# A graph-attention layer and a top-p attention layer on one core: layer 1 put in order by a list scheduler at build time instead of written plans, with the buffers at the seam of the layers shared

## The chip, the core and the metric

The kernel runs on 1 core of one Trainium2 chip. The metric is the device time of one execution in microseconds (us). Five queues run side by side: PE (matrix products), DVE and ACT (element-wise work), POOL (small column work) and SP, which here only issues DMAs. Each queue runs its own instructions in order and waits on semaphores for the others. The inputs' transposed adjacency is laid out before the launch.

## The reference

There are N = 3327 nodes with D = 256 features and a symmetric 0/1 adjacency matrix. Two pre-normalised layers follow each other:

```python
# layer 0: graph attention, 4 heads of 64 features
h = relu(layernorm(x))
support = h @ weight                      # per head
w = leaky_relu(f1[m] + f2[n], 0.2) on the edges; attn = softmax over neighbours
x = x + attn @ support + bias + h @ proj_w.T + proj_b
# layer 1: two steps of a row-normalised graph sum R and of top-p attention A
X = relu(layernorm(x));  R = (adj + eye) / row sums
for n in range(2):
    A = top_p(softmax((Xa @ W1.T @ W2.T) @ (Xa @ W3.T).T), 0.9)   # rows cut to 90% of the mass, renormalised
    Xf = R @ Xf;  Xa = A @ Xa
    Z += Xf @ U1[n].T + Xa @ U2[n].T
x = x + layernorm(X + Z) * ln_g + ln_b
```

`A` is N x N and dense before the cut, so both steps make all 3327 x 3327 logits, find each row's threshold and multiply the cut matrix with `Xa`.

## The kernel before

Rows are cut into NT = 26 tiles of 128 (the last has 127). Layer 0 walks the adjacency in four column blocks of 6, 8, 8 and 4 tiles (`BLOCKS`), and within each over the 26 row tiles j; it makes attention weights on DVE (L588), sums features and weights on PE (L596, L606), and writes each adjacency tile it has read to a DRAM copy `adj_r` from POOL's queue, which layer 1 reads. When a block ends, its output tiles (class `Out`) are divided, normalised, turned (transposed), made into keys and queries, and multiplied with `U1` (`graph`, L524) to give the rows `xf` of layer 1's graph sum. The outputs of blocks 0 to 2 run between the next block's products; those of the last block run in a loop after the main loop (L700 to L720), where only they are at work.

Layer 1 has two steps s. In each, each row tile i goes through this chain (`Rows`):

- logits in 7 pieces of 512 columns (PE, L826) into three PSUM banks, copied to `lg` by ACT or DVE (`evict`, L837);
- `exp` (ACT, L849), a first `guess` of the threshold (POOL), four probes (ACT, L907: a whole row each, with its sum), each followed by small steps on ACT and DVE (`aim`, `go_on`, `narrow`), then `threshold`;
- on DVE `low` (L964), `largest` (L973), `last_kept`, and `keep` (L1012), which cuts the row; `make_sure` on POOL;
- in 7 groups g of four column tiles: transposes on PE (L1025), copies by ACT or DVE (L1035), products with the features `xa` into one bank (PE, L1046);
- in step 0: scale, transpose, query and key of the next step, the small products with `U2` (L1089) and stores to DRAM; in step 1: norm and output.

Beside that runs the graph sum, 26 tiles x 7 parts a step: a part loads four 128x128 tiles of `adj_r` into one of three `adjt` buffers (SP, L748) and multiplies them with `xf`, as a high and a low half (L769, L770). When a tile's seven parts are done, `add`, and in step 0 `high` and `low`, finish it.

What a step needs of the one before: the keys of all tiles (the first 24 come back from DRAM in one load, the last two are put in directly), all `xf` rows for any graph part, and all `xa` rows for any product. The four `xf` buffers are reloaded in place from POOL's queue (`load_graph`), once step 0's graph sum is finished.

The order in layer 1 is written out: `PLANS` holds three lists for each step (for the first tiles, the middle, and the last), each a row of words such as `m.evict.v.2` (role, operation, engine, piece). A loop over n from -3 to NT + 2 walks the list; the roles sit at fixed distances (`ROLES`: m is a tile ahead, c two behind), so that one pass of the list serves several tiles. The word `graph` takes parts of the graph sum at a rate that `PARTS` sets: 3, 7 and 8 parts in the first passes of step 0, and 6, 10 and 7 in those of step 1. `in_traced_order` (L127) then ties PE, DVE, ACT and POOL to the order in which the program was written; SP's DMAs are not tied, and the tile framework places them.

```python
ROLES = {"m3": -3, "m2": -2, "m": -1, "a": 0, "b": 1, "c": 2, "d": 3}
PARTS = ({-3: 0, -2: 0, -1: 3, 0: 7, 1: 8}, {-3: 0, -2: 0, -1: 6, 0: 10, 1: 7})
for s in range(STEPS):
    for n in range(-3, NT + 3):
        plan = plans[0 if n < 2 else 1 if n < NT else 2]
```

Layer 0 and layer 1 have SBUF and PSUM pools of their own: layer 1's are opened when layer 0's are closed.

Of the kernel before, what the change touches and what calls it, by code (L numbers as in the profile page):

```python
# [21 lines left out]
P = 128  # L22
D = 256
# [27 lines left out]
ROOT = 1 / 64  # L51


@with_exitstack
def kernel(
# [71 lines left out]
    def in_traced_order(begin):  # L127


        last = {}  # L130
        for ins in nc.cur_bb.bb.instructions[begin:]:
            if ins.engine not in ORDERED:
                continue
            if ins.engine in last:
                tc.add_manual_dep(
                    ins,
                    last[ins.engine].name,
                    mybir.DependencyInfo(
                        mybir.DependencyClass.NoSync, mybir.DependencyReason.DATA
                    ),  # L140
                    reason="traced order",
                )
            last[ins.engine] = ins
# [45 lines left out]
    def queries_and_keys(xt, i, s, ptag, keys):  # L189
# [10 lines left out]
        yield from hi_and_lo(t, pq, i, s)  # L200
        nc.sync.dma_start(
# [7 lines left out]
    def new_keys(pool):  # L209
        k_sb = pool.tile([2 * DA, N + 1], FR, tag="k_sb", name="k_sb")  # L210
        return k_sb, small.tile([2 * DA, 2], FP, tag="mean", name="mean")
# [16 lines left out]
    def load_graph(pool, s):  # L228
        xf = new_graph(pool)
        for g0, g1 in SPREADS:  # L230
            if s == 0:
                ones_of_graph(xf, g0, g1)
            for t0, t1 in ((g0, min(g1, NF)), (max(g0, NF), g1)):
                if t0 < t1:
# [3 lines left out]
                    for v in range(2):  # L238
                        move_rows(
                            nc.gpsimd,  # L240
                            xf[b][:, c : c + t1 - t0, v * DX : v * DX + D].bitcast(FP),
                            xf_d[s][n0:n1, v].rearrange("(t p) d -> p t d", p=p), p,
                        )
        return xf

    def part_of_keys(s, part):
        n = (EARLY if s else BLOCKS[-1][0] - 2) * P
        return ((0, n), (n, N))[part]
# [17 lines left out]
    def mean_of_keys(keys, s, part):  # L266
# [4 lines left out]
            mean[:, part : part + 1], k_sb[:, n0:n1].bitcast(FP), AX.X, ALU.add  # L271
        )
        if part == 1:
            nc.vector.tensor_scalar(
                k_sb[:, N:], mean[:, :1], mean[:, 1:], 1.0 / N, ALU.add, ALU.mult
            )

    EARLY = NT - 2

    def load_u(pool):  # L280
        u_sb = pool.tile([P, DC, 2, D], FP, name="u_sb")
# [26 lines left out]
    keys = new_keys(right)  # L308
    first_traced = len(nc.cur_bb.bb.instructions)
    with ExitStack() as l0:  # L310
        p0 = l0.enter_context(tc.tile_pool(name="p0", bufs=1))
        pa = l0.enter_context(tc.tile_pool(name="pa", bufs=2))
        ps = l0.enter_context(tc.tile_pool(name="ps1", bufs=1, space=PSUM))

        def bank(k, shape):
            return ps.tile(shape, FP, tag=f"b{k}", name="pt")

# [31 lines left out]
        sup = p0.tile([P, NT, D], FP, name="sup")  # L349
# [22 lines left out]
        def normalize(i):  # L372
            normed[i] = hn = pa.tile([P, D], FP, tag="x1", name="hn")
# [4 lines left out]
        def turn(i, k):  # L378
# [6 lines left out]
            hT = pa.tile([P, DC, P], FP, tag="hT", name="hT", bufs=4)  # L385
# [3 lines left out]
        def features(i, k):  # L389
# [9 lines left out]
            if i == t0:  # L399
                made["ef"] = pa.tile([H, 4, P], FP, tag="ef", name="ef", bufs=1)  # L400
            nc.scalar.activation(eas[:, i], f1, AF.Exp, scale=SLOPE)
            nc.scalar.activation(cf[:, i], f1, AF.Exp, scale=1.0 - SLOPE)
            nc.scalar.activation(made["ef"][:, i - t0], f2, AF.Exp, scale=SLOPE - 1.0)
            if i == t1 - 1:
                spread(t0, t1, made["ef"])
# [26 lines left out]

        class Out:
# [10 lines left out]
            def normalize(r):  # L444
# [5 lines left out]
                x1 = pa.tile([P, D], FP, tag="x1", name="x1")  # L450
# [33 lines left out]
            def turn(r, k):  # L484
# [6 lines left out]
                r.hT = pa.tile([P, DC, P], FP, tag="hT", name="hT", bufs=4)  # L491
# [28 lines left out]
            def graph(r, k):  # L520
# [10 lines left out]
                move_rows(nc.sync, p_d[r.n0 : r.n0 + pn], xu, pn)  # L531

            def take_graph(r):
# [6 lines left out]
                ones_of_graph(xf0, i, i + 1)  # L540
                for v in range(2):
# [6 lines left out]
        HP = H // 2  # L548
# [5 lines left out]
        for c in range(DC):  # L554
            for v, row in enumerate((u_row, v_row)):
                t = pa.tile([P, D], FP, tag="x1", name="wx")
# [14 lines left out]
        w1n = p0.tile([DA, DC, P], FP, name="w1n")  # L571
# [9 lines left out]
        def weigh(j, at, b, cn, *heads):  # L581
            pj = rows(j)
            for h in heads:
                ws[h] = w = pa.tile([P, CH], FP, tag="w", name="w", bufs=7)
# [29 lines left out]
        def load_adj(b, j):  # L614
            c0, pj = BLOCKS[b][0] * P, rows(j)
            cn = min(BLOCKS[b][1] * P, N) - c0
            ats[b, j] = at = pa.tile([P, CH], FP, tag="at", name="at", bufs=4)
# [11 lines left out]
        for step, (b, j) in enumerate(order):  # L629
# [41 lines left out]
            ot = pa.tile([P, HP + 1, CH], FP, tag="ot", name="ot", bufs=1)  # L671
# [5 lines left out]
            if b < NB - 1:  # L677
                last = b == NB - 2
                for k, r in enumerate(outs):
# [10 lines left out]
                    for when, f in (  # L690
                        (a + 1, r.output),
                        (a + (5 if last else 4), lambda r=r: (r.take_keys(), r.store_keys())),
                        (g + 1, r.take_graph),
# [6 lines left out]
        mean_of_keys(keys, 0, 0)  # L700
        n = len(outs)
        free = [3, 4, 5, 6, 7, 0, 1, 2]
        for k, r in enumerate(outs):
            r.divide(free[k])
        for k in range(n + 2):
            if k < n:
                outs[k].normalize()
            if 0 <= k - 2:
                outs[k - 2].keys(free[k - 2])
            if k < n:  # L710
                outs[k].relu()
            if 0 <= k - 2:
                outs[k - 2].take_keys()
            if 0 <= k - 1 < n:
                outs[k - 1].turn(free[n + k - 1])
        for k, r in enumerate(outs):
            r.graph(free[n + k])
            r.take_graph()
            r.store_keys()
            r.store()  # L720


    pl = ctx.enter_context(tc.tile_pool(name="pl", bufs=1))
    lng = row_of(pl, ln_g, "lng")
    lnb = row_of(pl, ln_b, "lnb")

# [10 lines left out]
    def graph(i, s, xf, ends):  # L737


        pn, n0 = rows(i), i * P  # L740
        acc = ps.tile([P, DX], FP, tag="accr", name="accr")
        dx = D if s else DX
        for g in range(NG):
            c0 = 4 * g
            a = pw.tile([P, 4, P], FR, tag="adjt", name="adjt", bufs=ADJ)
# [10 lines left out]
            if g == 3:  # L756
                while ends:
                    ends.pop(0)[1]()
                ad = pw.tile([P, D], FP, tag="ad", name="ad", bufs=1)
                move_rows(nc.sync, ad, (z_d if s else p_d)[n0 : n0 + pn], pn)  # L760

            todo = [(a[: rows(c0 + j), j, :pn], c0 + j) for j in range(cn)]
            if g == 0:
                todo.insert(0, (ident_r[:pn, :pn], i))
            for n, (w, c) in enumerate(todo):
# [3 lines left out]
                nc.tensor.matmul(acc[:pn, :dx], w, xc[:, :dx], start=begin, stop=False)  # L769
                nc.tensor.matmul(acc[:pn, :D], w, xc[:, DX:], start=False, stop=end)  # L770
            if g < NG - 1:
                yield

        def add():
            if s == 0:
                nc.vector.reciprocal(rdeg[:pn, i : i + 1], acc[:pn, D : D + 1])
            nc.vector.scalar_tensor_tensor(
                ad[:pn], acc[:pn, :D], rdeg[:pn, i : i + 1], ad[:pn], ALU.mult, ALU.add
            )
            if s == STEPS - 1:  # L780
                move_rows(nc.sync, r_d[n0 : n0 + pn], ad, pn)

        def high():
            nc.scalar.copy(hl[:pn, 0], ad[:pn])

        def low():
            nc.vector.tensor_tensor(hl[:pn, 1], ad[:pn], hl[:pn, 0].bitcast(FP), ALU.subtract)
            move_rows(nc.sync, xf_d[s + 1][n0 : n0 + pn], hl.bitcast(FP), pn)

        ends.append(("dve", add))  # L790
        if s < STEPS - 1:
            hl = pw.tile([P, 2, D], FR, tag="hl", name="hl", bufs=1)
            ends += [("act", high), ("dve", low)]
        yield
# [3 lines left out]
    class Rows:  # L798
# [6 lines left out]
        def __init__(r, i, s):  # L805
            r.i, r.s, r.pn, r.n0 = i, s, rows(i), i * P
# [12 lines left out]
        def logits(r, k_sb, *pieces):  # L819
            pn = r.pn  # L820
            for p in pieces:
# [9 lines left out]
        def evict(r, copy, *pieces):  # L831
            for p in pieces:
                if p == 0:
                    r.lg = pw.tile([P, N + 1], FP, tag="lg", name="lg", bufs=3)
# [4 lines left out]
        def exp(r):  # L839
            pn = r.pn  # L840
            sc = small.tile([P, 13], FP, tag="sc", name="sc", bufs=4)
# [6 lines left out]
            r.e = pw.tile([P, N], FP, tag="e", name="e", bufs=3)  # L848
# [4 lines left out]
        def guess(r):  # L853
# [8 lines left out]
            r.ends = small.tile([P, 2, 2], FP, tag="ends", name="ends", bufs=4)  # L862
            r.at = small.tile([P, 5], FP, tag="at", name="at", bufs=4)
# [25 lines left out]
        def aim(r, j):  # L889

            pn = r.pn
            r.ea = small.tile([P, 1], FP, tag="ea", name="ea")
            nc.scalar.activation(r.ea[:pn], r.at[:pn, 4:], AF.Exp, bias=r.c2[:pn], scale=-1.0)
            r.aims = []
            for by in (BELOW[j],) if j < PROBES - 1 else (BELOW[j], NEAR):
                aim = small.tile([P, 1], FP, tag="aim", name="aim")
# [5 lines left out]
        def probe(r):  # L902

            pn = r.pn
            r.g = small.tile([P, 1], FP, tag="g", name="g")
            junk = pw.tile([P, N], F8, tag="junk", name="junk", bufs=1)
# [13 lines left out]
        def narrow(r, j):  # L920
# [12 lines left out]
            mk = small.tile([P, 2], U32, tag="mk", name="mk")  # L933
# [7 lines left out]
            t = small.tile([P, 4], FP, tag="t", name="t")  # L941
# [13 lines left out]
        def threshold(r):  # L955
            r.th = small.tile([P, 1], FP, tag="th", name="th")
# [4 lines left out]
        def low(r):  # L961
            pn, e = r.pn, r.e[: r.pn]
            r.below = small.tile([P, 1], FP, tag="below", name="below")
# [11 lines left out]
        def last_kept(r):  # L975
# [3 lines left out]
            top = small.tile([P, 1], FP, tag="top", name="top")  # L979
# [16 lines left out]
            r.vm = small.tile([P, 2], FP, tag="vm", name="vm")  # L996
# [12 lines left out]
        def keep(r):  # L1009
            pn, e = r.pn, r.e[: r.pn]  # L1010
            kept = small.tile([P, 1], FP, tag="kept", name="kept")
# [3 lines left out]
            r.rk = small.tile([P, 1], FP, tag="rk", name="rk", bufs=4)  # L1015
# [14 lines left out]
        def copy_transposed(r, copy, *groups):  # L1030
            for g in groups:
                pt = r.pt.pop(g)
                r.wt[g] = wt = pw.tile([P, 4, P], FP, tag="wt", name="wt", bufs=WT)
# [60 lines left out]
        def store_features(r):  # L1094
            y = pw.tile([P, D], FP, tag="y_or_x1", name="y", bufs=1)
            nc.scalar.copy(y[: r.pn], r.pz[: r.pn, 1])
            move_rows(nc.sync, xa_d[r.s + 1][r.n0 : r.n0 + r.pn], y, r.pn)

        def store_sum(r, xa):
            zt = pw.tile([P, D], FP, tag="nxa_or_rt", name="zt", bufs=1)  # L1100
# [403 lines left out]
```

## Time and profile before

| | |
|---|---|
| median of 3 runs | 2077.71 us (2077.64 to 2079.32) |
| profiled execution | 2080.33 us, of which the span from first to last instruction is 2078.5 |
| PE / weight loads / DVE / ACT / POOL busy | 1988.8 / 1391.1 / 1710.0 / 1271.3 / 790.6 us |
| mean granted PE clock | 0.981 |
| layer 0's main loop ends | 656 us |
| first exp and first transpose of layer 1 | 689.9 and 738.0 us |
| last A product of step 0 ends, first transpose of step 1 | 1398.7 and 1456.8 us |
| last A product of step 1 ends | 2068.1 us |

The busy share is an average over stages with different limits, and PE's busy time is modelled with overlapping matmuls, so the stages have to be read one by one. In rows of the form "engine line operation out<-in", L is a line of the kernel; a bracket gives the idle time before the instruction and what ended it.

### The profile page before, as it was taken

Reading aid. Unit: us, or ns where it says so; the run is one execution under the profiler, and the core shown is the slowest. Engines: PE = TensorE matmul, PEld = TensorE weight load, DVE = VectorE, ACT = ScalarE, POOL = GpSimd, SP = SyncE. Lnnn points to the kernel's source line nnn. Section 1 sums busy time; section 2 is a strip of 40 time slices with the busy share of each in tenths; the row PEclk is TensorE's granted clock in tenths of the full one; section 3 lists DMA queues with packets and bytes.
Section 4 is the critical chain, followed back from the end, with each engine's and each line's share of the span. In section 5 each row is a group of like instructions: output and inputs, shape, how many; then the busy total and the mean of one; then the engine's idle time right before and its main releaser. Section 6 shows DMA issues by size and latency. Waiting matters only on the chain.

```text
span 2078.5 us, 34250 instructions
## 1 busy us (share of the span) xinstructions
PE 1988.8 (96%) x11474; PEld 1391.1 (67%) x11474; DVE 1710.0 (82%) x4055; ACT 1271.3 (61%) x1950; POOL 790.6 (38%) x1860
## 2 busy tenths in 40 slices
PE   7999999999998689999999999997999999999996
PEld 3343333233223578888888888876798898888885
DVE  5767888988886488888888888855899999999985
ACT  2110100101112788888888888838899999999982
POOL 3221231223332244444444444423554445544441
PEclk9999999999998899999999999999899999999998
DMA  5455556565564433333333333377244343344320
GB/s 180 140 163 175 196 191 226 168 217 191 171 190 138 136 86 101 102 96 99 103 98 103 102 100 103 102 220 206 64 105 117 104 108 95 101 106 111 99 74 20
DMA packets 318881, 270.60 MB, mean 130 GB/s; under 512 B 30200, under 2 KB 293879, under 8 KB 318568
## 3 DMA queue, kind: packets, MB, share of 16 engines
q1 hardware_dynamic: 304024, 216.04, 37.7%
q0 software_dynamic: 13504, 51.62, 7.0%
q8 instruction: 92, 1.51, 0.3%
q14 instruction: 93, 0.76, 0.1%
q10 hardware_dynamic: 1168, 0.67, 0.1%
HBM read 177.79 MB, written 88.62 MB: 128 GB/s over the span
## 4 chain that ended last, share of the span: by engine, by line
PE 49%; ACT 12%; DVE 3%; issue 2%; DMA 1%; POOL 0%; SPq 0%; ACTq 0%; DVEq 0%; POOLq 0%
PE acca L1046 23%; ACT junk L907 7%; PE pt L1025 6%; PE pg L826 6%; PE accr L769 5%; PE accr L770 5%; ACT e L849 2%; PE pz L1089 2%; DMA adjt<-adj_r 1%; ACT lg L837 1%; ACT aim L897 1%; DVE v L973 1%; ACT wt L1035 1%; PE pq L195 0%; PE pt L524 0%
## 5 line engine op out<-in xcount | busy, mean ns | idle before, releaser
L907 ACT ACTIVATE junk<-lg,at 128x3327 fp8e4<-128x3327 f32 (+1 forms) x208 | 637.8, 3067 | 13.0 <-POOL at L873 10.6
L588 DVE SCALAR_TENSOR_TENSOR w<-xf,cf,at 128x1024 f32<-128x1024 f32 (+4 forms) x416 | 425.6, 1078 | 52.3 <-PE pt L606 51.7
L769 PE MATMUL accr<-xf,adjt 128*128 128x258 f32 (+3 forms) x1352 | 367.8, 305 | 19.1 <-DMA adjt<-adj_r 15.3
L770 PE MATMUL accr<-xf,adjt 128*128 128x256 f32 (+1 forms) x1352 | 341.9, 285 | 0.0
L596 PE MATMUL pt<-w,sup 128*64 128x512 f32 (+5 forms) x1456 | 337.5, 576 | 1.1 <-DVE w L588 1.0
L1046 PE MATMUL acca<-xa,wt 128*128 128x256 f32 (+2 forms) x1352 | 317.9, 384 | 2.9 <-ACT wt L1035 2.9
L1046 PE MATMUL acca<-res,wt 128*128 128x256 f32 (+2 forms) x1352 | 317.8, 380 | 0.0
L769 PEld LDWEIGHTS accr<-xf,adjt 128*128 128x128 f32 (+1 forms) x1352 | 260.0, 192 | 29.5 <-DMA adjt<-adj_r 18.9
L1046 PEld LDWEIGHTS acca<-xa,wt 128*128 128x128 f32 (+2 forms) x1352 | 252.2, 192 | 36.0 <-ACT wt L1035 3.9
L1046 PEld LDWEIGHTS acca<-res,wt 128*128 128x128 f32 (+2 forms) x1352 | 247.7, 190 | 30.4 <-issue 0.7
L770 PEld LDWEIGHTS accr<-xf,adjt 128*128 128x128 f32 (+1 forms) x1352 | 260.8, 193 | 5.7
L826 PE MATMUL pg<-k_sb,q 128*128 128x512 f32 (+2 forms) x728 | 243.4, 427 | 15.4 <-DVE lg L837 6.7
L596 PEld LDWEIGHTS pt<-w,sup 128*64 128x64 f32 (+1 forms) x1456 | 95.2, 136 | 206.7 <-issue 136.8
L847 POOL TENSOR_SCALAR sc<-sc 128x1 f32<-128x1 f32 (+1 forms) x156 | 29.3, 216 | 510.1 <-ACT sc L845 510.1
L1025 PE MATMUL pt<-ident,e 128*128 128x128 f32 (+1 forms) x1352 | 194.5, 277 | 19.2 <-DVE e L1012 13.5
L973 DVE MAX8 v<-lg 128x8 f32<-128x416 f32 (+2 forms) x416 | 209.9, 577 | 0.1
L1025 PEld LDWEIGHTS pt<-ident,e 128*128 128x128 f32 (+1 forms) x1352 | 163.9, 145 | 60.1 <-ACT wt L1035 17.1
L964 DVE SCALAR_TENSOR_TENSOR lg<-e,th 128x3327 f32<-128x3327 f32 (+1 forms) x52 | 191.1, 3676 | 4.2 <-ACT th L957 4.2
L1012 DVE SCALAR_TENSOR_TENSOR e<-e,vm 128x3327 f32<-128x3327 f32 (+1 forms) x52 | 191.2, 3678 | 0.1
L1035 ACT COPY wt<-pt 128x512 f32<-128x512 f32 (+2 forms) x268 | 142.7, 545 | 57.9 <-PE pt L1025 41.2
L849 ACT ACTIVATE e<-lg,sc 128x3327 f32<-128x3327 f32 (+1 forms) x52 | 159.7, 3072 | 29.4 <-issue 26.9
L606 PE MATMUL pt<-w,eas 128*32 128x512 f32 (+5 forms) x1456 | 166.6, 568 | 0.0
(179 smaller groups left out, 2660.1 us busy)
## 6 DMA issues: line engine op xcount, KB each, us to landing
adjt<-adj_r SPq DMA_DIRECT2D x300, 256.0 KB, 3.1
at<-in_adj_t_dram SPq DMA_DIRECT2D x50, 512.0 KB, 5.9
adj_r<-at POOLq DMA_DIRECT2D x50, 512.0 KB, 5.3
at<-in_adj_t_dram SPq DMA_DIRECT2D x25, 384.0 KB, 3.2
adj_r<-at POOLq DMA_DIRECT2D x25, 384.0 KB, 3.5
qk_d<-qk SPq DMA_DIRECT2D x50, 128.0 KB, 2.2
q<-qk_d SPq DMA_DIRECT2D x100, 64.0 KB, 2.5
xf_d<-xf SPq DMA_DIRECT2D x50, 128.0 KB, 3.8
```

Source lines behind the costliest of these rows:

```text
L588: nc.vector.scalar_tensor_tensor(o, cb, cf[:pj, j, h : h + 1], a, ALU.max, ALU.mult)
L596: nc.tensor.matmul(acc[q * O : (q + 1) * O, :mn], sup[:pj, j, h * O : (h + 1) * O], ws[h][:pj, 512 * m : 512 * m + mn], start=(j == 0), st ...
L769: nc.tensor.matmul(acc[:pn, :dx], w, xc[:, :dx], start=begin, stop=False)
L770: nc.tensor.matmul(acc[:pn, :D], w, xc[:, DX:], start=False, stop=end)
L826: nc.tensor.matmul(r.pg[p][:pn, :mn], r.q[:, v, :pn], k_sb[:, m0 : m0 + mn], start=(v == 0), stop=(v == 1),)
L849: nc.scalar.activation(r.e[:pn], r.lg[:pn, :N], AF.Exp, bias=nmu[:pn], accum_out=r.ssum[:pn])
L907: nc.scalar.activation(junk[:pn], r.lg[:pn, :N], AF.Exp, bias=r.at[:pn, 4:], accum_out=r.g[:pn], saturate=False,)
L964: nc.vector.scalar_tensor_tensor(r.lg[:pn, :N], e, r.th[:pn], e, ALU.is_lt, ALU.mult, accum_out=r.below[:pn])
L973: nc.vector.max(r.v8[:pn, q], r.lg[:pn, q * w : min((q + 1) * w, N)])
L1012: nc.vector.scalar_tensor_tensor(e, e, r.vm[:pn, 1:], e, ALU.is_ge, ALU.mult, accum_out=kept[:pn])
L1025: nc.tensor.transpose(r.pt[g][: rows(c), j, : r.pn], r.e[: r.pn, c * P : c * P + rows(c)], ident[: r.pn, : r.pn],)
L1046: nc.tensor.matmul(r.acc[: r.pn], wt[: rows(c), j, : r.pn], xa[: rows(c), c, :], start=(c == 0), stop=(c == NT - 1),)
```

## The change

The written plans, `ROLES`, `PARTS` and the loop over them are gone. A class `Order` holds all operations of layer 1, both steps together, as tasks: the engines that can do each with a duration, what it depends on, the buffers that it takes from a ring and what gives them back, a latency to its users, and a priority (tile number plus an offset for its kind, `PLACES`). DMAs are tasks of SP. `run` is a greedy list scheduler: among the ready tasks it takes the earliest start, and among equal starts the smallest priority; a copy that ACT or DVE can do goes to whichever ends it first. The kernel is then emitted in the order of the planned starts, and from the end of layer 0's main loop on SP is tied to that order too. Graph parts have priorities that trail their tile (`TRAIL`).

The resulting order, by the built program: 31 graph parts stand before the first transpose of layer 1, 169 of 182 before the first product of step 0's tile 25; the other 13, and nine of step 1, stand between the last product of step 0 and the first transpose of step 1; in step 1, 178 stand before the products of tile 24. Between them the logits of the first four tiles of step 1 are made (six pieces before the last products of step 0). ACT does 521 copies out of PSUM of layer 1 in place of 470, DVE 259 in place of 310.

The end of layer 0 is written out by hand as `end_of_layer_0`: the first two tiles' logits, exp and guess are interleaved with the last four outputs, whose stores move behind their key transfers. For that, the buffers of layer 1 exist from the start and layer 0 uses them as its own: `lg` and `spare`/`weights`, `sup` and the `e` buffers, `at4` (adjacency rows) and `wt`, `junk`, `ad`, `u_sb`. One set of eight PSUM banks (`Banks`) serves both layers. `hT` has two buffers in layer 0 for four. `xf`'s reload is cut by block (`load_block`) and issued from SP; each block waits for the graph parts that use it. Small column tiles have 5 buffers. The loads of `ln_g` and `ln_b` come late in step 0.

```diff
+PLACES = {"E": -2.11, "M": 0.88, "SF": 0.93, "AD": 1.14, "TH": 0.98, "LS": 2.27, "F": 0.18, "A": -0.7, ...
+TRAIL = (2.7, 0.49)
+PATIENCE = {"PE": 0, "DVE": 0, "ACT": 0.15}
+class Order:
...
+        R = dict(q=3, lgb=3, lgs=3, e=3, tr=2, wt=3, acca=1, accr=2, adjt=3, ad=1, hl=1, nxa=1, y=1, xaT=1, qks=1)
...
+                    A(K("L", x), [("PE", 0.46 if x < 6 else 0.26)], d, pr(s, i, "L"), take=[("lgb", K("L", x), [K("E", x)])] + ...
+                    A(K("E", x), [("ACT", 0.50 if x < 6 else 0.3), ("DVE", 0.61 if x < 6 else 0.36)], [K("L", x)] + ([K("E", 0)] if x else []), pr(s, i, "E"))
+                A(K("X"), [("ACT", 3.3)], [K("E", x) for x in range(NP)] + ([("X",) + before] if before else []), pr(s, i, "X"), take=[("e", K(), [K("T", g) for g in range(NG)])])
+                A(K("G"), [("POOL", 3.7)], [K("X")], pr(s, i, "G"))
+                A(K("P", 1), [("ACT", 3.08)], [K("G")], pr(s, i, "P"))
...
+                    A(K("AL", g), [("SP", 0.45 if g < 6 else 1.3)], [], pr(s, i, "GP") + p.lag[s] - 1 + g * 0.001, take=[("adjt", K("AL", g), [K("GP", g)])], lat=2.7, order=[pal])
...
+                    A(K("GP", g), [("PE", (0.97 + (0.25 if g == 0 else 0)) if g < 6 else 0.5)], [K("AL", g)] + ([prev] if prev else []) + xd, pr(s, i, "GP") + p.lag[s] + g / 7,
...
+            e = min(cands, key=lambda z: min(c[0] for c in cands[z]))
+            m = min(c[0] for c in cands[e])
+            lim = m + tol.get(e, 0.0)
+            c = min((c for c in cands[e] if c[0] <= lim + 1e-9), key=lambda c: (c[1], c[0]))
...
+    slots = {
+        "lg": list(lgs),
+        "e": [both[:, k * (N + 1) : k * (N + 1) + N] for k in range(2)],
+        "adjt": [adjt[:, k] for k in range(3)],
...
-        for k in range(n + 2):
-            if k < n:
-                outs[k].normalize()
...
-    PLANS = (
...
+        def end_of_layer_0():
+            first, second = (new_tile(0, i) or tiles[0, i] for i in (0, 1))
+            for g in range(3):
+                sums[0, 0].load(g)
...
+            outs[0].normalize()
+            for p in range(3):
+                logits(first, p, "s")
+            outs[1].normalize()
+            outs[0].relu()
+            for p in (3, 4):
+                logits(first, p)
...
+            outs[0].graph(4)
+            logits(first, 5, "s")
+            outs[1].graph(5)
+            for part in (1, 2):
+                mean_of_keys(keys, 0, part)
+            logits(first, 6, "v")
+            first.exp()
...
+            outs[2].graph(6)
+            logits(second, 4, "s")
...
+        begun = len(nc.cur_bb.bb.instructions)
+        end_of_layer_0()
+        l0.close()
...
+        order = Order(PATIENCE, TRAIL, offs=PLACES)
+        order.run(*tail_state())
+        for _, key, engine in order.order:
...
+            emit(key[0], engine, *key[1:])
+        in_traced_order(first_traced, ORDERED)
+        in_traced_order(begun, (E.SP,))
```

## The prediction

> **What bounds the kernel now.** I read the page's busy rows first, then the stretches of 40 us, then the chain of waits, and last the order of time around the three places where the stretches sag. Page: the engines' shares, PE's busy tenths, the granted clock.
>
> ```profile
> span 2078.5 us, 34250 instructions
> PE 1988.8 (96%) x11474; PEld 1391.1 (67%) x11474; DVE 1710.0 (82%) x4055; ACT 1271.3 (61%) x1950; POOL 790.6 (38%) x1860
> ...
> PE   7999999999998689999999999997999999999996
> ...
> PEclk9999999999998899999999999999899999999998
> ```
>
> PE looks full everywhere, but its busy time overlaps (matmul ends are modelled), so I pace it: each form costs its start-to-start step in the dense stretch. An A product (L1046) steps 0.216 us, a graph matmul (L769, L770) 0.12, a logits matmul 0.23, a transpose 0.11, a small product (L1089) 0.43. Counting instructions at these steps gives 1293 us of PE work in the 1422.5 us after 656 (end of layer 0's main loop). The other 129.6 are PE idle or at a low clock: 49.0 in 656 to 800, 37.3 in 1345 to 1500, 17.1 in 1500 to 2000, 26.5 after; nothing in 820 to 1340. The stretches (PE, PEld, DVE, ACT, POOL busy, clock, DMA) show the same three sags:
>
> ```profile
> 680.00:720.00 40.00, 25.08 (x123) 19.64 (x122) 13.91 (x45) 28.14 (x34) 13.90 (x50) 0.89 0.53 141
> ...
> 1000.00:1040.00 40.00, 40.00 (x239) 34.62 (x239) 34.81 (x94) 36.12 (x54) 17.05 (x48) 1.00 0.39 103
> ...
> 1440.00:1480.00 40.00, 30.53 (x158) 25.48 (x159) 32.18 (x89) 33.44 (x43) 17.90 (x43) 0.83 0.31 80
> ...
> 1560.00:1600.00 40.00, 39.97 (x242) 35.60 (x242) 37.60 (x108) 37.31 (x53) 15.92 (x46) 1.00 0.41 107
> ...
> 2000.00:2040.00 40.00, 31.11 (x159) 26.11 (x158) 35.58 (x106) 28.01 (x38) 12.00 (x32) 0.90 0.13 35
> ```
>
> The chain of waits (start, length, what) gives the pace: in step 0 one A product of every tile stands 25.97 us after the last tile's, and PE holds the chain; in the second half of step 1 ACT holds it, every 23.98.
>
> ```profile
> 821.98 1.73 PE acca L1046 x8
> ...
> 847.95 1.73 PE acca L1046 x8
> ...
> 1734.94 3.17 ACT e L849 x2
> ...
> 1759.00 3.16 ACT e L849 x2
> ```
>
> The order of time shows the sags' causes: layer 1's first logits start after all four graph products of layer 0 and after its pools close; then a tile's chain (exp, guess, four probes, threshold, cuts, L1012) runs with too little for PE to do, and again at the change of steps.
>
> ```profile
> 672.58 9.07 PE L524 MATMUL pt<-ug,hT 128*128 128x512 f32 x16
> 682.85 1.67 PE L826 MATMUL pg<-k_sb,q 128*128 128x512 f32 x6 [1.20 <-DVE xf L537]
> ...
> 738.02 1.93 PE L1025 MATMUL pt<-ident,e 128*128 128x128 f32 x8 [3.62 <-DVE e L1012]
> ...
> 1456.80 1.97 PE L1025 MATMUL pt<-ident,e 128*128 128x128 f32 x8 [5.85 <-DVE e L1012]
> ...
> 2034.37 1.19 PE L1025 MATMUL pt<-ident,e 128*128 128x128 f32 x8 [4.06 <-DVE e L1012]
> ```
>
> **A rule against this reading.** The Trainium skill ("Perfetto Trace Analysis", Identifying the Most-Contended Engine) says to judge PE's headroom by its weight loads' busy share, not by its matmuls'. That is 34.6 of 40 at 1000, so 13% would be free inside steady stages too: some 125 us of 960, and a better order would end near 1915. The row of starts says otherwise: 8 A products take 1.73 us with 8 loads of 0.19 in them, 89% loads at full pace. I take the pace: a steady step 0 holds nothing.
>
> **The change, part by part.** Layer 0's main loop keeps its order on PE, ACT, DVE and POOL to its end at 656 (views in place of tiles; hT falls from 4 to 2 buffers, but transposes of neighbouring outputs are 2.6 steps apart and the one two back has had its last use): 0.
>
> (a) Start of layer 1. Pieces 0 to 4 of the first tile's logits now stand in the holes of layer 0's last chain, and two of the four graph products come after piece 6. What is left behind the last key split (DVE ends 673.6): its DMA (1.1 issue, 1.7 landing), two small DVE sums 0.5, piece 6 and its copy 0.8, the minus 0.2: exp at 678 where it was 689.9. From exp to the first transpose stood 48.1 us; with the second tile's exp (3.3) earlier I allow 50: 728 against 738.0. Up to there the new PE order holds layer 0's rest (10 us), 28 logits pieces (12) and 31 graph parts (a part is 4 weights x 2 matmuls, 0.926 on average: 28.7), so 51 of 72 us. Are the parts fed? Three adjt buffers, 3.1 to land, about 1.45 a part: 31 in 45 of the 48 us from 680. Idle 21, and 5 for the ramp (was 6.3): 26 for 49. Gain 23. Also gone from this place: the two parameter rows' loads (0.36 and 0.43 of SP), now late in step 0.
>
> (b) Rest of step 0. The old plan did 18 graph parts before n=2; now 32 are done before tile 0's A product and 169 before tile 25's, so 5.5 a tile: PE needs 3.0 logits + 2.9 transposes + 11.2 A + 2.3 small + 5.1 graph = 24.5 a tile for 25.97. ACT's and DVE's busy time per tile is 22.7 and 22.5 (35 of 40), 93% of 24.5, where a fixed order costs waits: I put 0.25 a tile, 6 in all (0 to 20). The end of tile 25's A product (1398.7) moves by 23 + 5.6 (idle 1345 to 1398.7, now filled) + 12 (13 graph parts left for later) - 2.8 (six pieces of step 1 pulled ahead) - 6 = 32, to 1367.
>
> (c) Change of steps. From that end to the first transpose of step 1 stood 58.1 us: 8.8 to exp (scale, query, key DMA, mean, last piece), 49.3 to L1012's end. The new order changes none of these operations; I keep 58 (52 if all contention goes, 66 if more). PE has 34.3 us of work in it now and 32 then (22 pieces, 22 graph parts, tile 25's small products), so what was filled is filled with other things: gain 0. Here the reload of xf (18 DMAs, 6.8 MB) moves from POOL to SP, and to a place behind tile 25's graph parts, which by the pace of (a) end some 27 us into the gap; before, it ran 1357.6 to 1388 beside tiles 24 and 25. Of xf's and of xa's instructions in this stretch (ns min/median/max, first and last start):
>
> ```profile
> L152 POOL DMA_DIRECT2D xf<-xf_d x18: 516/750/893, 1357.6 to 1379.2; - x18
> ...
> L152 SPq DMA_DIRECT2D xa<-xa_d x9: 303/498/596, 1405.3 to 1431.2; - x9
> ```
>
> By the skill ("DMA: Bandwidth & Descriptors", Issuing engines are not separate DMA queues) the queue that issues only changes the issue time, usually small: 0. By the rows 18 issues of some 0.5 us, like xa's, are 9 us of SP between adjt loads that graph parts wait for (24.9 us of such waits in this stretch). I take 0, since PE has 26 us to spare before the first transpose, and keep 8 for the range. With 6.8 MB in some 25 us it lands by 50; nine graph parts of step 1 stand ahead of that transpose in PE's order, so landing after 58 would hold the chain.
>
> (d) Step 1, first transpose to tile 24's (1456.8 to 2034.4, 577.6): PE gets 24 tiles x 14.1, 22 x 3.0 of logits and 169 graph parts, 561 us. In step 1 copies from PSUM are 10.3 a tile on ACT and 3.7 on DVE for 9 and 5: ACT 22.4 + 0.6 = 23.0, DVE 22.4 - 0.8 = 21.6, PE 23.4. Waits as in 1500 to 2000 (17.1 of 500) would make 580, none 561: I take 573, gain 4.5 (range +16 to -12).
>
> (e) The end. From tile 24's L1012 18 us to tile 25's (DVE 13 of them), 14 of transposes and products, 10.3 of norm, output and the last test: 44.1 before, and nothing here is removed. That graph parts now fill it frees no time by itself, since DVE sets it. 0.
>
> SP's stores and loads are now in one fixed order with the rest. Behind a store that waits for DVE or ACT stand adjt loads, and PE behind those. Before, PE and its loads waited 18.9 + 15.3 us for adjt in all (of 1422); I leave that as it is.
>
> Sum: 32 + 0 + 4.5 + 0 = 36.5. The profiled execution took 2080.33 (span 2078.5 and 1.8 around it), the median is 2.6 less: 2077.7 - 36.5 = 2041.
>
> **The rivals.**
> 1. As summed, 2041, 0.62; its own range 2020 to 2062.
> 2. All of PE's idle time that can go goes: (b) without loss 6, (c) 52 for 58, (d) 563: 22 more, 2019. For it: nothing in the order but data makes PE wait in (d). Against: ACT at 98% of PE's need there. 0.18.
> 3. The durations that the list was made with miss the chip's, and each tile waits on several engines in turn: 0.6 us over 50 tiles, 30 us, 2071. For: PE, ACT and DVE are within 8% of one another in step 1, so no engine absorbs it. 0.10: 0.05 of it faster, 0.04 the same, 0.01 slower.
> 4. Slower: SP's one order. If an adjt load stands behind a store whose data come late, PE stands in its own fixed order until it lands. A load not yet issued costs its 3.1 us landing, of which three buffers hide all but about 1 to 2. At 0.73 us a tile over 50 tiles the 36.5 are used up; at 1.5 a tile the end is at 2041 + 75 = 2116. For: 468 adjt DMAs share SP with some 450 others in layer 1. Against: the waits of 34 us now, also in a single queue. 0.10.
> That the change does not do what it says hardly arises: the instructions' order is as described, the operations are the same.
>
> The range 2014 to 2074 leaves out 0.07 below and 0.13 above. About 0.2% (4 us) is what a measurement of this kernel tells from no change: faster 0.85, same 0.04, slower 0.11.
>
> **What would show it.** Right: first exp near 678; first transpose of layer 1 near 728 with graph parts 1.4 us apart before it; A products of step 0 24.5 to 25 us apart; last one of step 0 near 1367; 58 us to the next transpose; step 1 at 23.8. Wrong: waits of PE for adjt above 60 us in all; the chain holding ACT or DVE in step 0; graph products waiting for xf just ahead of step 1's first transpose; PE idle in the middle of step 0.

## The result, and the profile after

The changed kernel takes 2173.99 us (median of 4 runs, 2172.60 to 2176.26) against 2078.34 in the same session: ratio 1.0461, interval 1.0443 to 1.0479. That is 96 us slower, where I had forecast 37 us faster. The page of the changed kernel, with the shares of the chain that ended last, by engine, as its last line:

```profile
span 2170.5 us, 34306 instructions
PE 2006.3 (92%) x11474; PEld 1406.3 (65%) x11474; DVE 1693.0 (78%) x4006; ACT 1293.7 (60%) x2001; POOL 774.6 (36%) x1842
...
PE   7999999999997899999999999849899999999997
...
PEclk9999999999999999999999999969999999999998
...
PE 59%; POOL 13%; ACT 11%; DVE 8%; issue 5%; DMA 3%; SPq 0%; DVEq 0%; ACTq 0%; POOLq 0%
```

Every engine has about its old busy time (within 23 us), and POOL is even busy for 16 us less. Yet it holds 13% of the chain, where it held none:

```profile
PE 49%; ACT 12%; DVE 3%; issue 2%; DMA 1%; POOL 0%; SPq 0%; ACTq 0%; DVEq 0%; POOLq 0%
```

That is the chain's line of the kernel before (its chain covers two thirds of the span). The same stretches of the changed kernel as the prediction shows of the one before:

```profile
680.00:720.00 40.00, 23.42 (x147) 20.50 (x146) 15.84 (x57) 35.84 (x46) 13.10 (x47) 0.91 0.68 181
1000.00:1040.00 40.00, 40.00 (x229) 35.22 (x228) 36.20 (x106) 36.55 (x50) 17.20 (x51) 1.00 0.21 54
1440.00:1480.00 40.00, 27.99 (x160) 25.65 (x161) 27.87 (x85) 33.79 (x46) 12.93 (x32) 0.77 0.69 187
1560.00:1600.00 40.00, 37.63 (x238) 33.75 (x237) 35.59 (x98) 32.06 (x42) 20.33 (x49) 1.00 0.45 109
2000.00:2040.00 40.00, 37.62 (x233) 33.76 (x232) 34.55 (x100) 31.64 (x46) 18.15 (x41) 1.00 0.41 99
```

The sag at 1440 is still there, and step 1 is full no longer: at 1560, where PE had 39.97 of 40, PE, DVE and ACT are all below 38, and so they are at 2000. No engine sets the pace; a loop of waits does. The order of time at the three places that the prediction named:

```profile
738.76 1.03 PE L1289 MATMUL pt<-ident,sup 128*128 128x128 f32 x8
...
1469.69 1.03 PE L1289 MATMUL pt<-ident,e 128*128 128x128 f32 x8
...
2121.95 1.04 PE L1289 MATMUL pt<-ident,e 128*128 128x128 f32 x8
```

From the second to the third, 24 tiles of step 1, 652.3 us pass, where it was 577.6. The chain of waits shows the loop (start, length, what):

```profile
1812.02 0.22 POOL sc L1129
1812.32 0.57 POOL sc L1130
1812.88 4.00 POOL sc L1131
1816.95 0.20 POOL sc L1132
...
1818.85 0.20 POOL at L1137
1819.08 3.16 ACT at L1171 x2
...
1844.27 0.22 POOL sc L1129
...
1845.72 3.38 POOL sc L1132
...
1854.98 0.54 POOL ln_rs L386
1855.54 0.50 DVE rt L1380
1856.06 0.42 DVE rt L1381
1856.48 3.60 DVE lg L1228 x2
```

L1129 to L1137 are the nine small instructions that make the first probe's input (`at`); the probe is L1171. Each is normally 0.2 to 0.6 us, but in 23 of step 1's 26 tiles one of them takes 3.4 to 4.0. In the second tile shown the end of the guess then holds `ln_rs`, the norm's root of three tiles earlier, which stands behind it on POOL; DVE waits for that with the output (L1380), and the next long pass (L1228) stands behind the output. The waits (us in total, times, longest), of the changed kernel and, in the last line, ACT's for the first probe's input in the kernel before:

```profile
ACT at L1171 <- POOL at L1137: 79.7, 33, 4.2
...
DVE rt L1380 <- POOL ln_rs L386: 56.6, 24, 3.7
PEld accr L1031 <- DMA adjt<-adj_r: 46.7, 30, 9.9
PE accr L1031 <- DMA adjt<-adj_r: 46.0, 23, 9.7
...
ACT junk L907 <- POOL at L873: 10.6, 6, 3.7
```

What makes one POOL instruction long is seen in the order of time when DVE's rows are read beside POOL's. Changed kernel:

```profile
1812.79 3.69 DVE L1276 SCALAR_TENSOR_TENSOR sup<-sup,vm 128x3327 f32<-128x3327 f32 x1
1812.85 4.03 POOL L1131 TENSOR_TENSOR sc<-sc,consts 128x1 f32<-128x1 f32 x1
...
1818.85 0.19 POOL L1137 TENSOR_TENSOR at<-sc 128x1 f32<-128x1 f32 x1
...
1819.08 3.07 ACT L1171 ACTIVATE at<-lg,at 128x3327 fp8e4<-128x3327 f32 x1 [3.25 <-POOL at L1137]
```

Kernel before, same place in step 1:

```profile
1551.16 0.19 POOL L873 TENSOR_TENSOR at<-sc 128x1 f32<-128x1 f32 x1
...
1552.71 3.68 DVE L1012 SCALAR_TENSOR_TENSOR e<-e,vm 128x3327 f32<-128x3327 f32 x1
1553.19 3.29 POOL L879 TENSOR_SCALAR sc<-sc 128x1 f32<-128x1 f32 x1
```

A POOL column operation (128x1) that begins while DVE is in the keep (L1276, L1012) or in the cut below the threshold (L1228, L964) ends 0.05 to 0.43 us after that pass. These are the passes that read two SBUF operands of 3327 columns. In layer 1 of each trace 54 POOL column operations take over 1.4 us, and all 54 began inside such a pass (49 in keeps, 5 in cuts, in both kernels); no other takes over 0.73. Three more in the kernel before, and three in the changed one, began in the first 0.05 us of a pass and took their usual time; one in the changed kernel began in a pass's last 5 ns. So the stall is as frequent as before; what moved is what it hits. In step 1 before, `at` was ready 1.55 us ahead of the keep in the rows above, and the stall fell on the guess's tail. Of step 1's 26 guesses, 1 took over 5 us to `at` before, 23 do now (mean 3.50 and 6.36 us).

The Trainium skill states this ("SBUF — State Buffer", Who interferes with whom): a DVE instruction with two SBUF inputs contends with a GpSimd (POOL) instruction that reads SBUF, and the port pair that the two share is an exclusive lock, where the order of issue decides who blocks. The rows agree: the 54 stand still until the pass's end, and the few that began together with a pass may be those that came first. The list scheduler knows POOL and DVE as independent engines, with 3.7 us for a guess.

### The profile page after: what moved, and what is told of

Same layout as the page of the kernel before. It is cut to its first block, busy times and chain, and to the rows that moved or that the text cites. A ratio compares the mean times of both kernels' runs of the same rounds, so it can differ in the third digit from the quotient of the medians.

```text
span 2170.5 us, 34306 instructions
## 1 busy us (share of the span) xinstructions
PE 2006.3 (92%) x11474; PEld 1406.3 (65%) x11474; DVE 1693.0 (78%) x4006; ACT 1293.7 (60%) x2001; POOL 774.6 (36%) x1842
## 4 chain that ended last, share of the span: by engine, by line
PE 59%; POOL 13%; ACT 11%; DVE 8%; issue 5%; DMA 3%; SPq 0%; DVEq 0%; ACTq 0%; POOLq 0%
PE acca L1310 15%; PE pt L887 15%; PE pt L897 7%; ACT at L1171 7%; PE pt L1289 4%; POOL sc L1131 3%; PE pg L1092 3%; PE accr L1031 3%; PE accr L1032 2%; PE pt L679 2%; DVE lg L1228 2%; PE pt L810 2%; POOL sc L1132 2%; PE pz L1353 2%; DMA adjt<-adj_r 2%
## 5 line engine op out<-in xcount | busy, mean ns | idle before, releaser
L1171 ACT ACTIVATE at<-lg,at 128x3327 fp8e4<-128x3327 f32 (+1 forms) x208 | 637.7, 3066 | 80.2 <-POOL at L1137 79.7
L879 DVE SCALAR_TENSOR_TENSOR lg<-xf,cf,at 128x1024 f32<-128x1024 f32 (+4 forms) x357 | 368.3, 1078 | 45.4 <-PE pt L897 45.2
L887 PE MATMUL pt<-lg,sup 128*64 128x512 f32 (+3 forms) x1250 | 336.6, 576 | 1.1 <-DVE lg L879 1.1
L1310 PE MATMUL acca<-xa,at 128*128 128x256 f32 (+2 forms) x1352 | 336.7, 393 | 0.0
L1310 PE MATMUL acca<-res,at 128*128 128x256 f32 (+2 forms) x1352 | 324.8, 382 | 0.0
L1031 PEld LDWEIGHTS accr<-xf,adjt 128*128 128x128 f32 (+1 forms) x1352 | 261.9, 194 | 60.6 <-DMA adjt<-adj_r 46.7
L1310 PEld LDWEIGHTS acca<-xa,at 128*128 128x128 f32 (+2 forms) x1352 | 255.9, 198 | 31.7
L1310 PEld LDWEIGHTS acca<-res,at 128*128 128x128 f32 (+2 forms) x1352 | 248.6, 191 | 30.7
L1289 PE MATMUL pt<-ident,sup 128*128 128x128 f32 (+2 forms) x910 | 133.3, 280 | 44.5 <-ACT at L1299 35.1
L897 PE MATMUL pt<-lg,eas 128*32 128x512 f32 (+3 forms) x1250 | 166.4, 568 | 0.0
L1228 DVE SCALAR_TENSOR_TENSOR lg<-sup,th 128x3327 f32<-128x3327 f32 (+1 forms) x35 | 128.8, 3681 | 19.1 <-ACT th L1221 19.0
```

Of the source, the lines that this page charges most:

```text
L879: nc.vector.scalar_tensor_tensor(o, cb, cf[:pj, j, h : h + 1], a, ALU.max, ALU.mult)
L887: nc.tensor.matmul(acc[q * O : (q + 1) * O, :mn], sup[:pj, j, h * O : (h + 1) * O], ws[h][:pj, 512 * m : 512 * m + mn], start=(j == 0), st ...
L897: nc.tensor.matmul(acc[h * QP : (h + 1) * QP, :mn], eas[:pj, j, h : h + 1].to_broadcast([pj, QP]), ws[h][:pj, 512 * m : 512 * m + mn], sta ...
L1031: nc.tensor.matmul(r.acc[:pn, :dx], w, xc[:, :dx], start=begin, stop=False)
L1171: nc.scalar.activation(junk[:pn], r.lg[:pn, :N], AF.Exp, bias=r.at[:pn, 4:], accum_out=r.g[:pn], saturate=False,)
L1228: nc.vector.scalar_tensor_tensor(r.lg[:pn, :N], e, r.th[:pn], e, ALU.is_lt, ALU.mult, accum_out=r.below[:pn])
```

## The experiments

Theory A: this stall in front of `at`. Theory B: SP's one order with adjt loads behind other transfers. Theory C: the list's durations are short everywhere. In the diffs, the long pass is shown for the keep; the cut is changed alike, and the way into the general path is closed.

**1. The two passes with one SBUF operand**, in the changed kernel and, as a control, in the kernel before.

```diff
-            nc.vector.scalar_tensor_tensor(
-                e, e, r.vm[:pn, 1:], e, ALU.is_ge, ALU.mult, accum_out=kept[:pn]
+            nc.vector.tensor_scalar(
+                e, e, r.vm[:pn, 1:], None, ALU.is_ge, ALU.add, accum_out=kept[:pn]
             )
```

> The changed kernel with one edit: the two long VectorE passes of a tile, the cut below the threshold and the last keep, read e once instead of twice (a compare with accumulation, without the product by e). Same length, same order on every engine; left out are the products, so that the kept weights are 0 or 1, and the way into the general path is closed. Theory A (POOL's guess stands still while such a pass with two SBUF inputs runs, before it has the input of the first probe): no POOL instruction above 1 us is left, the guess takes 3.7 us to that input instead of 7, step 1's A products go from 27.5 to 24.0-24.4 us a tile, and the whole ends 65 to 95 us earlier, 2080 to 2109. Theory B (SP's one order: adjt loads behind other transfers) and theory C (the list's durations are short everywhere, no single cause): within 10 us of 2174, pace 27 or more.

> The kernel before with the same edit of the two long VectorE passes (read e once, products left out, general path closed). A control: theory A holds that the written plan put the stall behind the input of the first probe in step 1, and that PE sets the pace in step 0, so it gains little: 2062 to 2079. If the one-input form is itself a cheaper pass, it gains here what it gains in the changed kernel, 50 us or more.

Changed kernel: 2064.05 us, ratio to before 0.9933 (0.9912 to 0.9954), so 110 us come back. Kernel before: 2076.62, ratio 0.9994 (0.9986 to 1.0003): nothing. The passes are as long as they were (mean 3.67 us against 3.68), so it is not a cheaper pass; and the control has the same changed values, so it is not these. The page of the changed kernel with that edit, and its order of time:

```profile
span 2060.4 us, 34306 instructions
PE 1972.2 (96%) x11474; PEld 1392.4 (68%) x11474; DVE 1690.9 (82%) x4006; ACT 1293.6 (63%) x2001; POOL 601.6 (29%) x1842
...
PE 89%; DMA 3%; ACT 3%; DVE 2%; issue 1%; POOL 1%; SPq 1%; POOLq 0%; DVEq 0%; ACTq 0%
```

```profile
1697.12 3.68 DVE L1276 TENSOR_SCALAR_CACHE_REDUCE sup<-sup,vm 128x3327 f32<-128x3327 f32 x1
...
1699.95 0.22 POOL L1138 TENSOR_SCALAR sc<-sc 128x1 f32<-128x1 f32 x1
...
1700.15 0.26 POOL L1139 TENSOR_SCALAR sc<-sc 128x1 f32<-128x1 f32 x1
```

POOL's instructions run inside the pass at their usual length: 488 column operations begin inside one, and none is above 0.73 us. `at` is there after 3.39 us, POOL has lost 173 us of busy time and PE holds 89% of the chain. Theory A is shown, and my estimate of its size (65 to 95) was too low. The stall was in the kernel before too, and cost it nothing.

The edit changes the form of the DVE instruction along with its operands. Shorter instructions in the changed kernel's trace tell the two apart. DVE's `scalar_tensor_tensor` of 128x256 with one operand in PSUM and one in SBUF (L1042, L1331) did not stall POOL: of 74 column operations that began more than 0.05 us into one, 39 ended inside it. With both operands in SBUF, in that form (L1377) or as a `tensor_tensor` (L1052), none of 22 did. So it is the second SBUF operand, not the form.

**2. SP free again.**

```diff
-        in_traced_order(begun, (E.SP,))
```

> The changed kernel without the fixed order on SP; PE, DVE, ACT and POOL keep theirs. Theory B: adjt waits of PE (46 us) fall below 20 and the time by 40 us or more. Theory A: the step-1 pace stays at 27 to 27.6 us a tile, and only the change of steps can gain, by 0 to 25 us: 2149 to 2180.

2168.77 us, ratio 1.0426 (1.0401 to 1.0451), which overlaps the changed kernel's interval. The waits for adjt fall only to 38.4 and 32.5 us, and the 24 tiles of step 1 take 654.6 us (652.3 in the changed kernel). Theory B is out as the main cause. (Freeing the order leaves SP one queue: the longest wait for adjt is still 8.6 us.)

**3. No reload of xf.**

```diff
-                xfs.setdefault(1, {})[s] = new_block(right, s)
-                load_block(xfs[1], 1, s, nc.sync)
+                xfs.setdefault(1, {})[s] = xf0[s]
```

> The changed kernel without the reload of xf at the change of steps: step 1 multiplies by step 0's xf, so the graph products' values are not those of the reference; no other transfer and no order is changed. Theory A leaves the step-1 pace at 27.5 and says that the reload is a separate loss: adjt loads stand behind it, graph parts behind those on PE, the add behind them on DVE, and step 1's first probes behind the add: 15 to 30 us at the change of steps, 2144 to 2159. If the reload is hidden, as I took it, nothing: 2174.

2161.85 us, ratio 1.0407 (1.0386 to 1.0429): 12 us, three less than the range's low end. From the last A product to step 1's first transpose it is 8.9 us less. So the reload is a second, smaller loss. The waits of the changed kernel between 1390 and 1500 show its way:

```profile
PEld accr L1031 <- DMA adjt<-adj_r: 27.7, 9, 9.9
...
DVE rdeg L1041 <- PE accr L1032: 27.2, 2, 14.3
...
ACT hl L1048 <- DVE at L1042: 15.7, 2, 9.2
```

and in the order of SP's queue, with DMA share and GB/s (last two columns) of the stretches:

```profile
1423.91 2.75 SPq L369 DMA_DIRECT2D xf<-xf_d  x4
1426.76 0.98 SPq L1010 DMA_DIRECT2D adjt<-adj_r  x2
```

```profile
1420.00:1440.00 20.00, 9.12 (x51) 8.03 (x50) 2.53 (x12) 11.71 (x15) 2.84 (x10) 0.67 1.02 295
1440.00:1460.00 20.00, 10.82 (x52) 9.71 (x52) 12.95 (x42) 15.95 (x19) 5.95 (x16) 0.67 0.94 264
```

An adjt load issued at 1426.76 lands 5.9 us later, behind the reload's bytes (median 3.1 elsewhere). PE stands in its order at that graph part, DVE at the sum behind it (L1041), ACT at the cast behind that (L1048), and in their fixed orders step 1's first `narrow` and probes stand behind those two. Without the reload the 27.7 us of the first line are 16.4.

Not all of that line is the reload's. Its longest wait, 9.9 us, ends at 1417, before the reload begins. The chain there runs through a load of `xa`, and behind that through an adjt load that SP issues late:

```profile
1404.81 9.11 DMA xa<-xa_d
1413.94 3.07 DMA adjt<-adj_r
```

Without the reload this wait is still there (8.8 us).

**4. Both edits, and the keep alone.**

> The changed kernel with the one-input passes (products left out, general path closed) and without the reload of xf (step 1 multiplies by step 0's xf). If the port and the reload are separate losses, the gains add: 110 + 9 to 13, so 2051 to 2055; if the reload's wait only shows behind the late probes, 2064.

> The changed kernel with the one-input form in the last keep alone; the cut below the threshold keeps its two inputs (the keep's product left out, general path closed). In the changed kernel's step 1 every stalled guess stood in a keep. If those are the loss, most of the 110 us goes here too: 2064 to 2085. If the guess then runs into the cut instead, less than half: above 2115.

Both: 2055.31, ratio 0.9890 (0.9865 to 0.9915). The gains add: the reload is worth 8.7 us in the one-input kernel too. The keep alone: 2069.34, ratio 0.9948 (0.9930 to 0.9966), so 105 of the 110 us are the keeps', which have 49 of the 54 stalls.

**5. The stall kept, the order made for it.** The offsets were found with a replay: the lists' orders run through with the tasks' durations, the stall and the transfers' rate. It is a way to an order, not a measurement.

```diff
-                A(K("G"), [("POOL", 3.7)], [K("X")], pr(s, i, "G"))
+                A(K("G"), [("POOL", 7.3)], [K("X")], pr(s, i, "G"))
...
-TRAIL = (2.7, 0.49)
+TRAIL = (-1.66, -12.45)
```

(and other `PLACES` and `PATIENCE`); then the same kernel with the one-input passes, and the length alone with the old offsets.

> The changed kernel, nothing left out: the list takes the guess as 7.3 us of POOL instead of 3.7 (what it takes with one stall in it), and its offsets, trail and patience are set anew, by a replay of the lists with the stall in it. The two-input passes stay. Theory A: the order now leaves room for the stalled guess, so step 1 goes from 27.4 to about 24.8 us a tile and the whole to 2085 to 2105, with the same number of stalls (about one a tile). If the loss came from the list's form itself (theory C), another set of offsets gains no more than 20 us: 2155 or more.

> The kernel of long_guess with the one-input passes (products left out, general path closed). Theory A: where the order has room for the stall, taking it away gains little, 2 to 15 us, against 110 in the changed kernel.

> The changed kernel with only the list's guess at 7.3 us instead of 3.7; offsets, trail and patience as they were. The replay with the stall gives 1.6 us more than for the changed kernel: the offsets were found for a short guess and don't fit. 2150 to 2195. If knowing the length is all that was missing: below 2110.

2086.32 us, ratio 1.0036 (1.0026 to 1.0045): 88 us back, with 54 stalls as before. ACT waits once for the first probe's input, 3.0 us; of step 1's guesses 7 take over 5 us to `at`. Without the stall the new order gains 8 us more (2078.02, ratio 0.9999, 0.9988 to 1.0010), against 110 in the changed kernel. So the new order is not simply a better one: without the stall it is 14 us behind the old (2064.05). The length alone: 2148.26 (two runs), ratio 1.0339 (1.0320 to 1.0358), 26 us back. So theory C falls too: with the list's form and its other durations as they were, step 1's keeps come about 24.5 us apart (27.4 in the changed kernel); one wrong entry, and offsets found for it, did the damage.

**6. The kernel before, with `at` made later.** Eight instructions of the guess that `at` doesn't need are put ahead of it.

```diff
-            g.tensor_tensor(at, r.cx[:pn], a0, ALU.subtract)
             g.tensor_scalar(tgt, ssum, TOP_P, None, ALU.mult)
             g.tensor_scalar(sw, rs, ssum, FAR * DENS, ALU.mult, ALU.mult)
...
+            g.tensor_tensor(at, r.cx[:pn], a0, ALU.subtract)
```

> The kernel before with eight small POOL instructions of the guess moved ahead of the one that makes the first probe's input (they don't need it; all results stay): that input comes some 2.2 us later. In the trace of before it is there 1.55 us ahead of the keep. Theory A: now it falls behind the keep's start and waits for its end, some 5 us a tile where ACT sets the pace (step 1): 2110 to 2190. Without a port only the 2.2 us count, where they count at all: 2078 to 2115.

> The kernel of late_first_probe_before with the one-input passes (products left out, general path closed): what the 2.2 us cost by themselves. Theory A: most of the loss of late_first_probe_before goes, 2077 to 2110, at least 30 us less than that kernel.

2131.40, ratio 1.0257 (1.0239 to 1.0274), and with the one-input passes 2082.54, ratio 1.0019 (1.0009 to 1.0030): the 2.2 us of work cost 4 us, and the stall 49. Waits and order of time of the first of the two:

```profile
ACT junk L907 <- POOL at L881: 92.3, 47, 5.7
```

```profile
1553.83 3.68 DVE L1012 SCALAR_TENSOR_TENSOR e<-e,vm 128x3327 f32<-128x3327 f32 x1
1553.93 3.63 POOL L878 TENSOR_TENSOR ends<-sc 128x1 f32<-128x1 f32 x1
...
1557.87 0.18 POOL L881 TENSOR_TENSOR at<-sc 128x1 f32<-128x1 f32 x1
1558.09 3.08 ACT L907 ACTIVATE junk<-lg,at 128x3327 fp8e4<-128x3327 f32 x1 [0.28 <-POOL at L881]
```

The size was as expected, the place was not. In step 1 the input is late, as forecast, but ACT has another probe to do until then and waits 0.28 us: the keeps stay 24.0 us apart (23.9 before). The loss is in step 0, 27.72 a tile for 25.80 (keeps 4 to 25), with 74.7 of the 92.3 us of waits. There 23 of 26 guesses of the kernel before were stalled ahead of `at` already, so the 2.2 us more seem to have used up the room that hid the stall.

**7. A list that knows the stall and the bytes.** Guess at 6.5 us; a transfer lands behind the bytes issued before it at 0.27 MB a us; offsets set anew.

```diff
+            if e == "SP":
+                moved = max(moved, st + d) + size[k[0]] / 0.27
+                T[k]["lat"] = max(T[k]["lat"], moved + 1.0 - st - d)
```

> The changed kernel, nothing left out: the list takes the guess as 6.5 us of POOL, and lets a transfer land behind all bytes issued before it on SP (0.27 MB a us, the rate of 1420 to 1440 in the changed kernel's trace; four issues of the reload at 4.3 us), and its offsets, trail and patience are set anew by the replay with the stall in it. Theory A with the reload as the second loss: 5 to 16 us below long_guess, 2068 to 2080, so 0.5% faster than before to equal with it. If neither matters any more there: as long_guess, 2086.

2074.68 us, ratio 0.9983 (0.9976 to 0.9990): 99 us below the changed kernel, and 4 us (0.2%) below the kernel before, which is as good as equal. Step 1's keeps are about 23.9 us apart, and `at` comes after 3.65 us on average in step 1. What the guess, the bytes and the offsets each gave of the 12 us below the kernel of experiment 5 was not tried.

## Why the prediction was wrong

By its own steps, in us (starts of the first transposes, end of the last A product), with the changed kernel without the stall beside it:

| step | predicted | changed kernel | one-input passes |
|---|---|---|---|
| (a) first transpose of layer 1 at | 728 | 738.8 | 735.3 |
| (b) from there to the last A product of step 0 | 639 | 655.7 | 632.9 |
| (c) to the first transpose of step 1 | 58 | 75.2 | 73.4 |
| (d) to tile 24's transpose | 573 | 652.3 | 570.2 |
| (e) to the end | 44.1 | 48.5 | 48.5 |

- **What failed is a term that the sum did not have.** I wrote that ACT, DVE and PE need 23.0, 21.6 and 23.4 us a tile in step 1, and gave POOL no line. The list moved POOL's guess against DVE's keep, and I followed neither. The sum took as nothing what the stalled guess holds up, in (d) and in (b). Without the stall (d) is 570.2 for 573 and (b) 632.9 for 639; the stall costs 82 us in (d), 23 in (b), and 5 in (a) and (c) together, no more than profiled executions of the same order differ by there.
- **(a)** The first exp came at 673.6, earlier than my 678, but its first transpose 65 us later instead of 50. The stall explains 3.5 us at most: the one-input kernel has it at 735.3, but the same order without stall and reload has it at 738.4. In the one-input kernel ACT stands 2.9 us in this stretch behind a cast that waits for a late graph sum; with the orders of experiments 5 and 7 the transpose is at 727.6 and 727.5. Which of their moves did that was not tried, so this step's miss stays open.
- **(b)** Right where the stall is gone: A products end at 1368.2 (1367 forecast) and keeps 4 to 25 are 24.72 us apart (24.75). In the changed kernel they are 25.46 apart, and the end hardly moves, 1394.5. The pacing of PE by start-to-start steps gave (b) and (d) within 7 us. The reading by weight loads, that some 125 us more are free, is not borne out by any order tried: at 1560 PE is busy 39.86 of 40 in the one-input kernel with weight loads at 35.83, and the fastest kernel here took 2055.31. That no order can get there is not shown.
- **(c)** The reload taken as 0 costs 7 to 9 us here, which is what I had kept for the range. I looked for graph parts waiting for xf; they waited for adjt loads behind xf's bytes, and DVE's and ACT's orders carried that on. The rule that I took for the 0 is about the queue that issues; no run had the reload on another queue, so whether the queue matters is not shown. Another 8 us over the 58 remain without the reload (66). The 8.8 us for which PE waits there for an adjt load that stands behind SP's loads of `xa` may be these; no run tested it.
- **(e)** 4.4 us more; kernels with the list's order have 2.6 to 4.4 more. In the one-input kernel's chain graph parts stand between the last A products. This was not tested by itself.
- **The rivals.** Rival 3, list durations that miss the chip's, was the right family and much too small: I spread 0.6 us over all tiles (2071), while one task was off by 3.6 us at the head of a loop. Rival 4, SP's one order, named the wrong queue: freeing SP gave 5 us, which is not clear of noise. Of my signs, waits for adjt above 60 us in all came true (46.7 + 46.0), and were not the cause: in the one-input kernel they are still 44.3 + 43.8. The true sign, the chain on POOL, was not on my list.

## What to carry to other kernels

A list scheduler that gives each engine its own clock must be told of what engines share: here a small POOL instruction that starts inside a DVE pass with two SBUF operands lasts until that pass ends. Ask of every step that moves not only what it waits for but what runs beside it in its new place, and give the idle-looking engine a line in the sum. A stall that costs nothing before (before's 54 stalls: ratio 0.9994 without them) is a debt that any reordering can call in.

## What the runs showed of the hardware

- A DVE pass that reads two SBUF operands stopped POOL's 128x1 operations until its end: 54 of 57 that began in it in the kernel before, 54 of 58 in the changed one, the rest having begun within 0.05 us of its start or at its very end. The same pass with one SBUF operand and an accumulated sum, equally long (3.67 us), stopped none of 488. `scalar_tensor_tensor` with one operand in PSUM did not stop POOL either (39 of 74 ended inside it).
- With the reload in SP's queue, DMA engines were at full share (1.02, 295 GB/s) between 1420 and 1440, and 256 KB loads of the same queue took 5.9 us and more to land instead of 3.1.
